# Single-row loads of a graph kernel: one even stream over the loop's slots, 58 row tiles in place of 60

## The chip, the core and the metric

The kernel runs on one core of a Trainium2 chip. A core has five engines, each with its own queue of instructions: TensorE (PE; its weight loads are shown apart as PEld), VectorE (DVE), ScalarE (ACT), GpSimd (POOL) and SyncE (SP). The last issues DMAs and computes nothing; ScalarE and GpSimd issue DMAs too. Engines wait for each other through semaphores. The metric is the time of one execution in microseconds on the device; the median of several runs is compared.

## What is computed

A graph layer with 6,250 nodes of 128 features, 206,250 edges sorted by receiver, and eight heads of 16:

```python
w_ij = silu(edge_feats @ rad_W1 + rad_b1) @ rad_W2 + rad_b2
w_ij = w_ij + (silu(chi_scalar @ sph_W1 + sph_b1) @ sph_W2 + sph_b2)
q_i = (node_feats @ Wq)[receivers]        # 8 heads of 16
k_j = (node_feats @ Wk)[senders]
alpha = (q_i * w_ij * k_j).sum(-1) / sqrt(16) * cutoffs[:, None]
v_j = (node_feats @ Wv)[senders]
out = segment_sum(alpha[..., None] * v_j, receivers) / 16
x = layernorm(x + out)
```

All in float32. The receivers are sorted, so a few neighbouring receivers share each tile; the senders are random, so keys and values have to be fetched edge by edge.

## The kernel before

**Tiles.** An edge tile is 128 edges, one to a partition. Four tiles are a quad (512 edges, 403 quads in all), four quads a group (101 groups). The setup computes keys and values of all nodes and stores them in device memory as `kv_tab`, one row of 1 KB per node. Then the main loop takes one quad per step; a step is called a slot here (`i`), and the quads of a group come in the order 0, 2, 1, 3 (`order`, line 147).

**A slot.** In slot `i` TensorE sums the messages of the group before (L664), computes the hidden layer of quad `i+2` (`first_layers`, L560), brings the queries of quad `i+1` to its edges (`q_at_edges`, L579) and computes the edge weights of quad `i+1` (`weigh`, L612). The last matmul of `q_at_edges` gives TensorE's one signal of the slot. ScalarE's first activation (L597), VectorE's product of query and key (`multiply`, L628) and GpSimd's gathers all wait for such a signal; the gathers issued in slot `i` wait for that of slot `i-1`. VectorE then multiplies by the edge weights (L636), reduces per head (L638) and forms the messages (L653). One reduction at L638 stands for one quad, so counts of quads can be read from it.

**Two ways of fetching keys and values.** Usually GpSimd fetches a tile with one indirect DMA of 128 rows (`gather`, L141): four per quad, issued 14 quads ahead, into a ring of 16 buffers. In 60 quads, spread evenly over quads 14 to 401 (`row_at`, six or seven quads apart), the fourth tile comes in another way: 128 single DMAs of one row each, 60 issued by SyncE and 68 by ScalarE. Such a quad has three gathers. Its fourth tile is a row tile; it lands in a buffer named `wide`, of which there are three in turn. For each DMA the row's byte offset must be in a register, and a load instruction (L208) reads up to 32 of them on SyncE and 24 on ScalarE; so a tile takes two loads on SyncE and three on ScalarE. The DMA itself is at L214. Before `multiply` of such a quad, VectorE waits for the count of all its rows and gathers (L625).

**How the rows are dealt.** `load_rows(i)` stands at the end of each slot. For the tile in turn it puts the rows and loads into a list per engine (`rows_left`), counts a load as `ROW_LOAD` units and a row as one, divides the tile's units over the slots from the previous tile's end to `row_at[k] - ROW_LEAD` (six or seven slots), and lets each engine take as many as it is owed. ScalarE keeps back two units (`ROW_CARRY`), which `copies` issues one by one between the activations of the next slot. SyncE has other work between the rows: node rows (L315), results (L773), receiver numbers (L263) and edge features (L252), one of them in each slot; the first and the last wait for a signal of TensorE two slots back.

Of the kernel before, what the change touches and what calls it, by code (L numbers as in the profile page):

```python
# [14 lines left out]
U8 = mybir.dt.uint8  # L15
# [6 lines left out]
SP = mybir.EngineType.SP  # L22
ACT = mybir.EngineType.Activation
WAIT = mybir.DependencyInfo(mybir.DependencyClass.Sync, mybir.DependencyReason.DATA)

P = 128
# [19 lines left out]
ROW_BYTES = 2 * D * 4  # L46
# [1 line left out]
MSGS = 10  # L48
ACTS = 8
RING = 16  # L50
ROW_TILES = 60
ROW_FIRST = 8
ROW_LAST = 401
ROW_LEAD = 5
ROW_ACT = 68
ROW_AT = {SP: 0, ACT: 64}
ROW_LOAD = 5
ROW_CARRY = 2
ROW_UNITS = {SP: 32, ACT: 24}
XU = 4  # L60
# [3 lines left out]
ROW_SEMS = 8  # L64
# [8 lines left out]
def gnn_kernel(ctx, tc, x, src, dst, weight, edges, rad_W1, rad_b1, rad_W2, rad_b2,  # L73
# [14 lines left out]
    nc = tc.nc  # L88
# [12 lines left out]
    src_x = const.tile([P, math.ceil(XQ / NQ) * GT], I32, name="src_x")  # L101
    at_i = const.tile([ROW_TILES, P + 4], I32, name="at_i")
    scale = const.tile([P, NT], F32, name="scale")
# [33 lines left out]
    def quad_of(name, bufs, width=D):  # L137
        return ep.tile([P, QT, width], F32, name=name, bufs=bufs)
# [8 lines left out]
    order = [g * NQ + j for g in range(NG) for j in (0, 2, 1, 3) if g * NQ + j < QUADS]  # L147
    row_at = [ROW_FIRST + (n + 1) * (ROW_LAST - ROW_FIRST) // ROW_TILES for n in range(ROW_TILES)]
    row_quads = {order[i] for i in row_at}
    row_of = {}  # L150
    row_done = {}
    rows_left = {SP: [], ACT: []}
    owed = {SP: 0, ACT: 0}
    row_work = {}
    row_issued = {}
    row_sems = [tc.alloc_semaphore(f"rows_{n}") for n in range(ROW_SEMS)]
    row_count = [0] * ROW_SEMS
# [4 lines left out]
    def next_rows(engine, n, loads=True):  # L162

        left = rows_left[engine]
        n = min(n, owed[engine])
        while n > 0 and left and (loads or left[0][0] == 1):
            cost, issue = left.pop(0)
            issue()
            n -= cost
            owed[engine] -= cost  # L170
# [19 lines left out]
        kv_of[q] = kv  # L190
        kv_done[q] = kv_sems[at], kv_count[at]

    def load_rows(i):

        k = next((k for k in range(ROW_TILES) if i <= row_at[k] - ROW_LEAD), None)
        start = None if k is None else (row_at[k - 1] if k else ROW_FIRST) - ROW_LEAD + 1
        if k is None or i < start:
            return next_rows(ACT, owed[ACT])
        q = order[row_at[k]]
        slots = row_at[k] - ROW_LEAD + 1 - start  # L200
        table = kv_tab.bitcast(U8).rearrange("(o n) b -> o (n b)", o=1)

        def rows_by(engine, name, a, b):
            regs = {}

            def load(e, m):
                c = ROW_AT[name] + e - a
                regs.update(zip(range(e, e + m), nc.values_load_multi_w_load_instructions(  # L208
                    at_i[k:k + 1, c:c + m], engines=(name,), min_val=0,
                    max_val=(N - 1) * ROW_BYTES,  # L210
                    skip_runtime_bounds_check_because="senders are nodes")[1]))

            def row(p):
                signalled(engine.dma_start(row_of[q][p:p + 1, 0, :].bitcast(U8),  # L214
                                           table[:, ds(regs.pop(p), ROW_BYTES)]))

            items = []
            for e in range(a, b, ROW_UNITS[name]):
                m = min(ROW_UNITS[name], b - e)
                items.append((ROW_LOAD, lambda e=e, m=m: load(e, m)))  # L220
                items += [(1, lambda p=p: row(p)) for p in range(e, e + m)]
            rows_left[name] += items
            return sum(cost for cost, _ in items)

        def signalled(o):
            tc.no_tile_sem_insts.add(o.ins.name)
            tc.add_to_no_dep_group(f"rows_{q}", o.ins)
            o.then_inc(row_sems[k % ROW_SEMS], 16)
            row_count[k % ROW_SEMS] += 16
            row_done[q] = row_sems[k % ROW_SEMS], row_count[k % ROW_SEMS]  # L230
            row_issued[q] = row_issued.get(q, 0) + 1

        n = P - ROW_ACT
        if i == start:
            row_of[q] = quad_of("wide", 3, P)[:, :2, :].rearrange("p t d -> p (t d)")[:, None, :]
            row_work[SP] = rows_by(nc.sync, SP, 0, n)
            row_work[ACT] = rows_by(nc.scalar, ACT, n, P)
        for engine, m in row_work.items():
            a, b = (math.ceil(m * j / slots) for j in (i - start, i - start + 1))
            owed[engine] += b - a  # L240
        next_rows(SP, owed[SP])
        next_rows(ACT, owed[ACT] - ROW_CARRY)

    def kv_parts(q, t):

# [93 lines left out]
    with tc.tile_pool(name="nodes", bufs=1) as nodes, \  # L339
# [76 lines left out]

        rows_f = nodes.tile([P, ROW_TILES], F32, name="rows_f")

# [6 lines left out]
        def turn_rows():  # L425
            pt = nps.tile([P, QT, P], F32, name="pt", bufs=3)
            nc.tensor.transpose(pt[:ROW_TILES, 0, :], rows_f, ident)
            n = P - ROW_ACT
            for a, b, at in ((0, n, ROW_AT[SP]), (n, P, ROW_AT[ACT])):
                nc.vector.tensor_copy(at_i[:, at:at + b - a], pt[:ROW_TILES, 0, a:b])  # L430

# [69 lines left out]
        n = len(chunks)  # L501
# [14 lines left out]
        work = [(k, n) for k, (c, n) in enumerate(chunks)] + [((q, "x"), QT) for q in quads_x]  # L516
        turn(*work[0])
        turn(*work[1])
        for i, (k, n) in enumerate(work):
# [5 lines left out]
            if i >= len(chunks):  # L525
                kv_of[k[0]] = kvs
                a, b = ((j - len(chunks)) * (math.ceil(NT / P) - 1) // XQ for j in (i, i + 1))
# [26 lines left out]
    with tc.tile_pool(name="ps", bufs=1, space=PSUM) as pp, tc.tile_pool(name="loop", bufs=1) as lp:  # L554
# [253 lines left out]
        for g in range(NG - 1):  # L808
            for slot, j in enumerate((0, 2, 1, 3)):
                q = g * NQ + j  # L810
                i = g * NQ + slot
# [63 lines left out]
                if g == NG - 2 and slot == 0:  # L875
                    n = nc.values_load(general, min_val=0, max_val=1)
                if g == NG - 3 and slot in (1, 3):
                    weigh_wide(order[slot // 2 - 3])
                if g == NG - 2 and slot == 1:
                    weigh_wide(order[-1])  # L880
                load_rows(i)
        g, (a, b, c) = NG - 1, order[-3:]
        first_layers(c)
# [224 lines left out]
```

## Time and profile before

| | |
|---|---|
| median of 3 runs | 2596.52 us (2588.82 to 2597.5) |
| the profiled execution | 2599.59 us, of which span 2597.7 us |
| mean granted TensorE clock | 0.837 |
| TensorE matmul busy | 2090.8 us (80%) |
| VectorE busy | 1525.9 us (59%) |
| ScalarE busy | 645.0 us (25%), issue of DMAs not counted |
| GpSimd busy | 1470.8 us (57%) |
| DMA | 307.18 MB, mean 118 GB/s |
| single-row DMAs | 4080 from ScalarE, 3600 from SyncE |
| gathers of 128 rows | 1520 |

How to read it: a group of instructions is given as line, engine, operation, output and inputs, count, then busy time and the mean of one in ns, then the engine's idle time just before them and what ended most of it. "remote" is a release that the profile cannot tie to an instruction, "issue" a stretch in which it sees no wait at all. A `q` behind an engine's name (SPq, ACTq) is its sequencer, which issues DMAs and waits and is not counted as busy. In a listing in order of time the columns are start, duration, engine, line and operation, with the idle time before it in brackets; equal neighbours are merged and counted.

### The profile page before, as it was taken

Reading aid. Unit: us, or ns where it says so; the run is one execution under the profiler, and the core shown is the slowest. Engines: PE = TensorE matmul, PEld = TensorE weight load, DVE = VectorE, ACT = ScalarE, POOL = GpSimd, SP = SyncE. Lnnn points to the kernel's source line nnn. Section 1 sums busy time; section 2 is a strip of 40 time slices with the busy share of each in tenths; the row PEclk is TensorE's granted clock in tenths of the full one; section 3 lists DMA queues with packets and bytes.
Section 4 is the critical chain, followed back from the end, with each engine's and each line's share of the span. In section 5 each row is a group of like instructions: output and inputs, shape, how many; then the busy total and the mean of one; then the engine's idle time right before and its main releaser. Section 6 shows DMA issues by size and latency. Waiting matters only on the chain.

```text
span 2597.7 us, 56700 instructions
## 1 busy us (share of the span) xinstructions
PE 2090.8 (80%) x15990; PEld 1744.9 (67%) x15990; DVE 1525.9 (59%) x3427; ACT 645.0 (25%) x1359; POOL 1470.8 (57%) x1564
## 2 busy tenths in 40 slices
PE   5678888888888788878888878888887888888787
PEld 4567677666767666666667667666766767676666
DVE  3456556656656555656656556555656556565567
ACT  1122222222222222222222222222222222222223
POOL 4456565655565565555556555555555555565540
PEclk7788888888888888888888797888788787887888
DMA  5543444434343343434434434444343343443331
GB/s 180 173 118 112 120 124 116 121 112 122 113 123 116 116 124 114 120 112 122 121 111 123 119 114 121 115 120 121 114 120 118 111 122 115 119 124 108 118 103 35
DMA packets 157219, 307.18 MB, mean 118 GB/s; under 512 B 42022, under 2 KB 91360, under 8 KB 156896
## 3 DMA queue, kind: packets, MB, share of 16 engines
q0 software_dynamic: 73984, 201.43, 27.2%
q1 hardware_dynamic: 72976, 97.35, 11.4%
q10 hardware_dynamic: 9936, 4.72, 0.8%
q8 instruction: 127, 2.08, 0.3%
q14 instruction: 196, 1.61, 0.2%
HBM read 289.88 MB, written 15.11 MB: 117 GB/s over the span
## 4 chain that ended last, share of the span: by engine, by line
PE 38%; issue 20%; SPq 13%; DVE 13%; another core or an unknown queue 10%; ACTq 5%; ACT 1%; DMA 0%; DVEq 0%
PE pw L612 17%; SPq L214 10%; PE pq L579 7%; PE ph L560 6%; ACTq L214 4%; PE po L664 3%; DVE kq L628 3%; DVE side L638 2%; DVE kq L636 2%; SPq L208 2%; PE pq L705 1%; ACT act L597 1%; PE pk L381 1%; PE pq L286 1%
## 5 line engine op out<-in xcount | busy, mean ns | idle before, releaser
L141 POOL DMA_INDIRECT kv<-kv_tab,src_i x1520 | 1436.9, 945 | 1042.9 <-remote 447.9
L612 PE MATMUL pw<-w,act 128*128 128x128 f32 x6448 | 1060.4, 324 | 109.1 <-issue 107.6
L612 PEld LDWEIGHTS pw<-w,act 128*128 128x128 f32 x6448 | 951.7, 231 | 187.0 <-issue 149.7
L597 ACT ACTIVATE act<-ph,b 128x512 f32<-128x512 f32 x806 | 554.7, 689 | 1843.5 <-remote 1374.7
L628 DVE TENSOR_TENSOR kq<-pq,kv 128x512 f32<-128x512 f32 (+1 forms) x404 | 270.6, 670 | 931.3 <-remote 680.0
L560 PE MATMUL ph<-feats,w 32*128 32x512 f32 x1612 | 665.7, 740 | 138.5 <-issue 128.8
L579 PE MATMUL pq<-q,hotT 32*128 32x128 f32 x3224 | 557.5, 321 | 20.9 <-issue 17.8
L579 PEld LDWEIGHTS pq<-q,hotT 32*128 32x128 f32 x3224 | 470.7, 220 | 33.0 <-issue 32.7
L560 PEld LDWEIGHTS ph<-feats,w 32*128 32x128 f32 x1612 | 190.7, 207 | 303.6 <-issue 272.0
L638 DVE TENSOR_REDUCE side<-kq 128x32 f32<-128x512 f32 x404 | 280.2, 694 | 14.0
L653 DVE TENSOR_TENSOR msg<-kv,side 128x512 f32<-128x512 f32 (+1 forms) x404 | 268.7, 665 | 13.9
L636 DVE TENSOR_TENSOR kq<-pw,kq 128x512 f32<-128x512 f32 x404 | 274.1, 679 | 0.0
L664 PE MATMUL po<-msg,hot 128*32 128x128 f32 x3200 | 183.2, 309 | 34.2 <-issue 34.1
L567 PE MATMUL pw<-brow,onesb 3*128 3x512 bf16 x403 | 176.5, 438 | 0.0
L664 PEld LDWEIGHTS po<-msg,hot 128*32 128x32 f32 x3200 | 84.5, 118 | 91.2 <-issue 63.6
L705 PE MATMUL pq<-part,to 128*128 128x128 f32 x196 | 56.6, 380 | 107.6 <-issue 54.4
L705 PEld LDWEIGHTS pq<-part,to 128*128 128x128 f32 x196 | 38.6, 245 | 122.2 <-issue 83.7
L641 DVE TENSOR_TENSOR side<-side,scale 128x32 f32<-128x32 f32 x400 | 79.7, 199 | 13.7
L381 PE MATMUL pk<-wkv,xT 128*128 128x256 f32 x162 | 45.6, 424 | 38.0 <-DVE kv L382 23.9
L292 DVE TENSOR_TENSOR hotT<-relb,side 128x512 f32<-128x512 bf16 x101 | 68.6, 679 | 0.0
L286 PE MATMUL pq<-wq,xT 128*128 128x128 f32 x200 | 49.6, 336 | 23.5 <-issue 15.9
L382 DVE COPY kv<-pk 128x512 f32<-128x512 f32 (+1 forms) x41 | 27.4, 682 | 68.9 <-remote 48.5
(126 smaller groups left out, 892.9 us busy)
## 6 DMA issues: line engine op xcount, KB each, us to landing
wide<-kv_tab ACTq DMA_DIRECT2D x4080, 1.0 KB
wide<-kv_tab SPq DMA_DIRECT2D x3600, 1.0 KB
feats<-in_edges SPq DMA_DIRECT2D x101, 512.0 KB
kv<-kv_tab,src_i POOLq DMA_INDIRECT x1520, 2.9
relb<-rel_four SPq DMA_DIRECT2D x101, 128.0 KB
x<-in_x SPq DMA_DIRECT2D x101, 64.0 KB
out<-y SPq DMA_DIRECT2D x101, 64.0 KB
kv_tab<-kv SPq DMA_DIRECT2D x12, 512.0 KB
```

Of the source, the lines that this page charges most:

```text
L141: return nc.gpsimd.indirect_dma_start(out=o, out_offset=None, in_=table, in_offset=bass.IndirectOffsetOnAxis(ap=index, axis=0))
L214: signalled(engine.dma_start(row_of[q][p:p + 1, 0, :].bitcast(U8), table[:, ds(regs.pop(p), ROW_BYTES)]))
L560: return nc.tensor.matmul(act_of[q, i], w1[r0:r0 + R, :], feats_of[g][r0:r0 + R, c0:c0 + EQ], start=True, stop=True)
L567: nc.tensor.matmul(pw, onesb[f:f + 3, :], brow[f:f + 3].rearrange("p t d -> p (t d)"), start=True, stop=False)
L579: o = nc.tensor.matmul(pq_of[q][:, t, :], hotT_of[g][b, t * P:(t + 1) * P], q_of[g][b, :], start=True, stop=True)
L597: o = nc.scalar.activation(act, act_of[q, i], AF.Silu, bias=b1[:, i:i + 1])
L612: o = nc.tensor.matmul(pw[:, t, :], act_of[q, i][:, t * P:(t + 1) * P], w2[:, i, :], start=False, stop=(t == QT - 1 and i == 1))
L628: o = nc.vector.tensor_tensor(kq_of[q][:, u, :], pq_of[q][:, u, :], kv[:, :, :D], op=OP.mult)
L636: nc.vector.tensor_tensor(m, pw_of[q][:, t, :], m, op=OP.mult)
L638: nc.vector.tensor_reduce(alpha, m.rearrange("p t (h e) -> p t h e", e=HD), AX.X, OP.add)
L653: nc.vector.tensor_tensor(msg_of[q][:, u, :].rearrange("p t (h e) -> p t h e", e=HD), kv[:, :, D:].rearrange("p t (h e) -> p t h e", e=HD) ...
L664: o = nc.tensor.matmul(po_of[g][j * W:(j + 1) * W, :], hot_of[g][:, j * QT + t, :], msg_of[g * NQ + j][:, t, :], start=(t == 0), stop=(t = ...
```

## The change

The rows and loads of all tiles now form one stream. `load_rows(i)` computes how many tiles, as a fraction, are due at slot `i`: (i − 8 + 6) · 58 / 393. Tiles are opened (buffer taken, list filled) in a new function `open_tile` when the stream reaches them, and each engine is owed the difference between what is due by now and what was dealt before. There are 58 row tiles instead of 60, six or seven quads apart (12 of the spacings are six, before 26); two of the quads that had a row tile now have a fourth gather. `ROW_LEAD` goes from 5 to 6, and a load counts as six units instead of five. Behind the last tile ScalarE keeps nothing back.

```diff
-ROW_TILES = 60
+ROW_TILES = 58
 ROW_FIRST = 8
 ROW_LAST = 401
-ROW_LEAD = 5
+ROW_LEAD = 6
-ROW_LOAD = 5
+ROW_LOAD = 6
...
-    def load_rows(i):
-
-        k = next((k for k in range(ROW_TILES) if i <= row_at[k] - ROW_LEAD), None)
-        start = None if k is None else (row_at[k - 1] if k else ROW_FIRST) - ROW_LEAD + 1
-        if k is None or i < start:
-            return next_rows(ACT, owed[ACT])
+    def open_tile(k):
+
         q = order[row_at[k]]
-        slots = row_at[k] - ROW_LEAD + 1 - start
+        row_of[q] = quad_of("wide", 3, P)[:, :2, :].rearrange("p t d -> p (t d)")[:, None, :]
...
         n = P - ROW_ACT
-        if i == start:
-            row_of[q] = quad_of("wide", 3, P)[:, :2, :].rearrange("p t d -> p (t d)")[:, None, :]
-            row_work[SP] = rows_by(nc.sync, SP, 0, n)
-            row_work[ACT] = rows_by(nc.scalar, ACT, n, P)
-        for engine, m in row_work.items():
-            a, b = (math.ceil(m * j / slots) for j in (i - start, i - start + 1))
-            owed[engine] += b - a
+        row_open.append({SP: rows_by(nc.sync, SP, 0, n), ACT: rows_by(nc.scalar, ACT, n, P)})
+
+    def load_rows(i):
+
+        tiles = min(max((i - ROW_FIRST + ROW_LEAD) * ROW_TILES / (ROW_LAST - ROW_FIRST), 0), ROW_TILES)
+        while len(row_open) < math.ceil(tiles):
+            open_tile(len(row_open))
+        for engine in owed:
+            due = sum(min(max(tiles - k, 0), 1) * work[engine] for k, work in enumerate(row_open))
+            owed[engine] += math.ceil(due) - row_dealt[engine]
+            row_dealt[engine] = math.ceil(due)
         next_rows(SP, owed[SP])
-        next_rows(ACT, owed[ACT] - ROW_CARRY)
+        next_rows(ACT, owed[ACT] - (ROW_CARRY if tiles < ROW_TILES else 0))
```

The file is one to three lines shorter behind the edit, so L214 is L211 after it and L597 is L596. Three places show what stands where. SyncE, slots 44 to 47, which begin with the node rows of group 14 (`x`); before:

```order
L315 DMA x<-in_x 128x512
L214 DMA wide<-kv_tab 1x1024 x8
L773 DMA out<-y_2251 128x512
L214 DMA wide<-kv_tab 1x1024 x10
L263 DMA relb<-rel_four 128x1x512
L214 DMA wide<-kv_tab 1x1024 x10
L252 DMA feats<-in_edges 128x1024
L208 TENSOR_LOAD at_i
L214 DMA wide<-kv_tab 1x1024 x7
```

and now:

```order
L314 DMA x<-in_x 128x512
L211 DMA wide<-kv_tab 1x1024 x4
L205 TENSOR_LOAD at_i
L772 DMA out<-y_2295 128x512
L211 DMA wide<-kv_tab 1x1024 x11
L262 DMA relb<-rel_four 128x1x512
L211 DMA wide<-kv_tab 1x1024 x11
L251 DMA feats<-in_edges 128x1024
L211 DMA wide<-kv_tab 1x1024 x6
```

The other work of a slot stands where it stood; the rows between it are a few more or fewer, and the loads of row numbers fall elsewhere. GpSimd, the gathers of the quads 59 to 66 of the order, a row per quad (numbers of buffers in the names); before:

```order
L141 DMA kv_5510<-kv_tab_60,src_i_67 128x256 x4
L141 DMA kv_5627<-kv_tab_60,src_i_67 128x256 x3
L141 DMA kv_5752<-kv_tab_60,src_i_67 128x256 x4
L141 DMA kv_5862<-kv_tab_60,src_i_67 128x256 x4
L141 DMA kv_5938<-kv_tab_60,src_i_67 128x256 x4
L141 DMA kv_6112<-kv_tab_60,src_i_67 128x256 x4
L141 DMA kv_6179<-kv_tab_60,src_i_67 128x256 x4
L141 DMA kv_6289<-kv_tab_60,src_i_67 128x256 x3
```

and now:

```order
L141 DMA kv_5487<-kv_tab_60,src_i_67 128x256 x4
L141 DMA kv_5557<-kv_tab_60,src_i_67 128x256 x4
L141 DMA kv_5670<-kv_tab_60,src_i_67 128x256 x4
L141 DMA kv_5794<-kv_tab_60,src_i_67 128x256 x3
L141 DMA kv_5903<-kv_tab_60,src_i_67 128x256 x4
L141 DMA kv_5974<-kv_tab_60,src_i_67 128x256 x4
L141 DMA kv_6146<-kv_tab_60,src_i_67 128x256 x4
L141 DMA kv_6212<-kv_tab_60,src_i_67 128x256 x4
```

The quads with three gathers come a little less often. ScalarE, the slot whose quad time has three gathers (slot 45 before, slot 47 now; `part` and `tot` are copies of the running sums, `y` is a result); before:

```order
L597 ACTIVATE act_105<-ph,b_73 128x512
L214 DMA wide<-kv_tab 1x1024
L709 ACTIVATE tot<-pq 128x128
L214 DMA wide<-kv_tab 1x1024
L597 ACTIVATE act_106<-ph,b_73 128x512
L742 ACTIVATE y_4026<-y_4026,shift,rs 128x128
L214 DMA wide<-kv_tab 1x1024
L208 TENSOR_LOAD at_i
L214 DMA wide<-kv_tab 1x1024 x6
```

and now:

```order
L596 ACTIVATE act_101<-ph,b_73 128x512
L211 DMA wide<-kv_tab 1x1024
L699 ACTIVATE part<-po 128x128
L211 DMA wide<-kv_tab 1x1024
L596 ACTIVATE act_102<-ph,b_73 128x512
L741 ACTIVATE y_4018<-y_4018,shift,rs 128x128
L211 DMA wide<-kv_tab 1x1024 x11
```

Nine rows and a load stood in that slot; thirteen rows and no load stand there now.

More of the change, by code (lines that the diff above doesn't have):

```diff
@@ L153, in gnn_kernel @@
     owed = {SP: 0, ACT: 0}
-    row_work = {}
+    row_dealt = {SP: 0, ACT: 0}
+    row_open = []
     row_issued = {}
@@ L213, in row @@
             def row(p):
-                signalled(engine.dma_start(row_of[q][p:p + 1, 0, :].bitcast(U8),
-                                           table[:, ds(regs.pop(p), ROW_BYTES)]))
+                o = engine.dma_start(row_of[q][p:p + 1, 0, :].bitcast(U8),
+                                     table[:, ds(regs.pop(p), ROW_BYTES)])
+                tc.no_tile_sem_insts.add(o.ins.name)
+                tc.add_to_no_dep_group(f"rows_{q}", o.ins)
+                o.then_inc(row_sems[k % ROW_SEMS], 16)
+                row_count[k % ROW_SEMS] += 16
+                row_done[q] = row_sems[k % ROW_SEMS], row_count[k % ROW_SEMS]
+                row_issued[q] = row_issued.get(q, 0) + 1
             items = []
@@ L223, in rows_by @@
             return sum(cost for cost, _ in items)
[L225 to L231, printed above, removed]
-        n = P - ROW_ACT
-        if i == start:
-            row_of[q] = quad_of("wide", 3, P)[:, :2, :].rearrange("p t d -> p (t d)")[:, None, :]
-            row_work[SP] = rows_by(nc.sync, SP, 0, n)
-            row_work[ACT] = rows_by(nc.scalar, ACT, n, P)
-        for engine, m in row_work.items():
-            a, b = (math.ceil(m * j / slots) for j in (i - start, i - start + 1))
-            owed[engine] += b - a
+        n = P - ROW_ACT
+        row_open.append({SP: rows_by(nc.sync, SP, 0, n), ACT: rows_by(nc.scalar, ACT, n, P)})
[7 more added lines that the diff above has]
+            row_dealt[engine] = math.ceil(due)
         next_rows(SP, owed[SP])
-        next_rows(ACT, owed[ACT] - ROW_CARRY)
+        next_rows(ACT, owed[ACT] - (ROW_CARRY if tiles < ROW_TILES else 0))
     def kv_parts(q, t):
```

## The prediction

> **What bounds the kernel now.** I read the page first, then the time order of GpSimd, then SyncE and VectorE at the quads with a row tile, and last the same rows in an early and a late stretch. The page's groups and its chain:
>
> ```profile
> span 2597.7 us, 56700 instructions
> PE pw L612 17%; SPq L214 10%; PE pq L579 7%; PE ph L560 6%; ACTq L214 4%; PE po L664 3%; DVE kq L628 3%; DVE side L638 2%; DVE kq L636 2%; SPq L208 2%; PE pq L705 1%; ACT act L597 1%; PE pk L381 1%; PE pq L286 1%
> L141 POOL DMA_INDIRECT kv<-kv_tab,src_i x1520 | 1436.9, 945 | 1042.9 <-remote 447.9 <-issue 352.0 <-PE pq L579 170.8
> L597 ACT ACTIVATE act<-ph,b 128x512 f32<-128x512 f32 x806 | 554.7, 689 | 1843.5 <-remote 1374.7
> ```
>
> No engine is full, and yet SyncE's issue of single rows (L214) is a tenth of the chain. GpSimd in order of time shows the beat. First an ordinary quad, then a quad with three gathers, then the rows that ScalarE issued in that short quad:
>
> ```profile
> 454.83 0.94 POOL L141 DMA_INDIRECT kv<-kv_tab,src_i  x1 [1.62 <-remote]
> 456.08 0.95 POOL L141 DMA_INDIRECT kv<-kv_tab,src_i  x1 [0.30 <-issue]
> 457.33 0.95 POOL L141 DMA_INDIRECT kv<-kv_tab,src_i  x1 [0.31 <-issue]
> 458.59 0.95 POOL L141 DMA_INDIRECT kv<-kv_tab,src_i  x1 [0.31 <-issue]
> 461.09 0.94 POOL L141 DMA_INDIRECT kv<-kv_tab,src_i  x1 [1.55 <-remote]
> ...
> 521.96 0.94 POOL L141 DMA_INDIRECT kv<-kv_tab,src_i  x1 [1.53 <-remote]
> 524.46 0.95 POOL L141 DMA_INDIRECT kv<-kv_tab,src_i  x1 [0.30 <-issue]
> 526.73 0.94 POOL L141 DMA_INDIRECT kv<-kv_tab,src_i  x1 [1.32 <-remote]
> ```
>
> ```profile
> 521.73 0.69 ACT L597 ACTIVATE act<-ph,b 128x512 f32<-128x512 f32 x1 [4.42 <-remote]
> 522.75 0.69 ACT L597 ACTIVATE act<-ph,b 128x512 f32<-128x512 f32 x1
> 522.82 3.51 ACTq L214 DMA_DIRECT2D wide<-kv_tab  x10
> 526.49 0.69 ACT L597 ACTIVATE act<-ph,b 128x512 f32<-128x512 f32 x1 [3.06 <-remote]
> ```
>
> Gathers start 1.25 us apart, and after each burst GpSimd, ScalarE and VectorE wait for TensorE's one signal, 1.3 to 1.6 us. Four gathers make a quad of 6.26 us (454.83 to 461.09), three make one of 4.77 us (521.96 to 526.73). So the number of gathers sets the beat. Now a late quad that takes its fourth tile from single rows:
>
> ```profile
> 2343.29 4.67 SPq L214 DMA_DIRECT2D wide<-kv_tab  x11
> 2349.36 0.56 DVE L628 TENSOR_TENSOR kq<-pq,kv 128x384 f32<-128x384 f32 x1 [6.97 <-issue]
> 2347.40 0.95 POOL L141 DMA_INDIRECT kv<-kv_tab,src_i  x1 [0.30 <-issue]
> 2354.82 0.94 POOL L141 DMA_INDIRECT kv<-kv_tab,src_i  x1 [6.47 <-PE pq L579]
> ```
>
> SyncE's last row of the tile goes out at 2347.96, VectorE has stood idle 6.97 us and starts 1.4 us later, TensorE gets the product's bank late, and GpSimd's next burst waits 6.47 us where 1.5 is usual. It was not always so. The last rows of an early tile, its use, and the same at the tile ten further on:
>
> ```profile
> 296.37 3.90 SPq L214 DMA_DIRECT2D wide<-kv_tab  x9
> 327.98 0.56 DVE L628 TENSOR_TENSOR kq<-pq,kv 128x384 f32<-128x384 f32 x1 [1.50 <-remote]
> 714.92 4.01 SPq L214 DMA_DIRECT2D wide<-kv_tab  x7
> 722.77 0.56 DVE L628 TENSOR_TENSOR kq<-pq,kv 128x384 f32<-128x384 f32 x1 [0.97 <-remote]
> ```
>
> The lead falls from 27.7 us (300.27 to 327.98) to 3.8 us (718.93 to 722.77) in 65 quads. SyncE cannot keep up with the rows; from there on it sets the mean pace. VectorE's waits in the late stretch (us in total, times, longest) say the same, as do the quads counted by their reductions in both stretches (206 to 723 and 723 to 2515 us):
>
> ```profile
> DVE kq L628 <- remote: 496.6, 202, 3.0
> DVE kq L628 <- DVEq L625: 48.0, 11, 6.4
> DVE kq L628 <- DMA wide<-kv_tab: 43.8, 8, 7.1
> DVE kq L628 <- issue: 30.9, 5, 7.0
> L638 DVE TENSOR_REDUCE side<-kq 128x32 f32<-128x512 f32 x85 | 59.1, 695 | 2.9
> L638 DVE TENSOR_REDUCE side<-kq 128x32 f32<-128x512 f32 x288 | 200.1, 695 | 10.0
> L141 POOL DMA_INDIRECT kv<-kv_tab,src_i x327 | 309.2, 945 | 207.6 <-remote 103.0 <-issue 75.2 <-PE pq L579 24.5
> L141 POOL DMA_INDIRECT kv<-kv_tab,src_i x1112 | 1051.2, 945 | 741.8 <-remote 332.3 <-issue 256.6 <-PE pq L579 136.8
> ```
>
> 517/85 = 6.08 us a quad early, 1792/288 = 6.22 late.
>
> **The change part by part.** (a) *The stall that can go.* 0.14 us a quad over 288 quads is 40 us. Two other readings bound it. GpSimd's idle time per gather rises from 207.6/327 = 0.635 to 741.8/1112 = 0.667 us, times 1112 is 36 us. VectorE's 24 waits for rows (48.0 + 43.8 + 30.9 = 122.7 us), less an ordinary wait of 496.6/202 = 2.46 us each, are 64 us. I take 40, the reading of the whole pace; ends 36 and 64.
>
> (b) *Does SyncE keep up now?* Need before: 60 rows per tile, 60 tiles on 393 slots, 9.16 rows a quad. After: 58 tiles, 8.855 rows a quad. Supply in the early stretch: ten tiles (600 rows) between the two ends above, 418.7 us, are 1.433 rows/us, times 6.08 us is 8.71 rows a quad. SyncE also loads row numbers twice a tile:
>
> ```profile
> L208 SPq TENSOR_LOAD <-at_i x120: 420/1932/2442, 137.9 to 2559.1; - x120
> ```
>
> Four loads fewer (two tiles at two) free 0.02 us a quad, 0.03 rows; the lower share of short quads adds about 0.01 row. Supply 8.75. The shortfall shrinks from 0.45 to 0.105 rows a quad, 0.073 us; over 393 quads 29 us, and the lead to be eaten is 27.7 us. So the rows become late only at the very end, if at all. A missing row cost 0.14/0.45 = 0.31 us. I take 1 us for what stays. Ends: nothing, and with 1% less supply a shortfall of 0.195 rows, which uses the lead up after 204 quads and costs 189 × 0.195 × 0.31 = 11 us.
>
> Two edits that the words of the change put first count for nothing in (b). "Six slots ahead" moves SyncE's end hardly at all: the old code deals a tile's last row in slot row_at − 5, the new one when the stream passes the tile, which by its formula is 4 to 5 slots before the multiplication, against 4; ScalarE gains one slot and was never late. And the even deal cannot help a queue that is behind, since it works through its entries in order anyway; it only spares ScalarE the slots with 14 rows. What brings the balance is the two tiles left out: 120 of 3,600 rows on SyncE.
>
> (c) *Two gathers more.* Two quads grow from three gathers to four: 2 × (6.26 − 4.77) = 3 us; by the 1.25 us between starts alone 2.5. I take 3.
>
> (d) *At nothing.* 136 fewer rows on ScalarE, at 3.51/10 = 0.35 us each 48 us of its queue: it idles 1374.7 us for TensorE's signal. If it were the bound instead of GpSimd, they would be a gain. Two pairs of 128-wide products on VectorE become parts of wider ones inside its 2.46 us waits, and two fewer conversions in the setup are a fraction of a microsecond. The new tiles' buffer (three of them) is written some seven slots after its last reader, so SyncE's first row of a tile waits no more than now; nothing that stands behind it (feature blocks, node rows, outputs) is held.
>
> Sum: −40 + 1 + 3 = −36 us. The profiled execution took 2599.6 us (2597.7 of it span), so 2563.6; it lies 3.1 us above the median of the runs, 2596.5, so 2560.5, said as 2561.
>
> One rule speaks to (b). SyncE's rows are quick in parts of a quad and slow in others; here four take 2.87 us although ScalarE issues only two beside them and then nothing until 1018.76:
>
> ```profile
> 1015.65 2.87 SPq L214 DMA_DIRECT2D wide<-kv_tab  x4
> 1015.67 0.55 ACTq L214 DMA_DIRECT2D wide<-kv_tab  x2
> 1018.76 0.69 ACT L597 ACTIVATE act<-ph,b 128x512 f32<-128x512 f32 x1 [5.04 <-remote]
> ```
>
> The Trainium skill, "Perfetto Trace Analysis", section "DMA Instruction — HWDGE (DVE, Sync)", has the descriptor generator shared by two issuing engines and locked for one at a time, the lock wait being part of the profiled time. By that SyncE would lose a fixed time per tile to ScalarE's rows and not a fixed time per quad; its late need, 1792 us for 2637/60 = 44 tiles or 40.7 us a tile, would fit well into 6.776 quads of 6.08 us, (b) would be 0 and the sum 1 us lower. The trace does not bear it out as the main cause, since the slow rows fall where ScalarE issues none.
>
> **The rivals.** *SyncE stays late.* Its supply is known from one stretch. At 2.4% less, 8.5 rows a quad, the shortfall is 0.355 rows, 0.25 us; the lead is gone after 112 quads, and 281 × 0.355 × 0.31 = 31 us of the stall stay: 2599.6 − 40 + 31 + 3 − 3.1 = 2590.5. For it: the lead's loss of 23.9 us over 65 quads, 0.37 us a quad, is a little more than 0.45 rows at 1.433 rows/us make (0.31). Against it, the late stretch, in which SyncE never rested:
>
> ```profile
> L214 SPq DMA_DIRECT2D wide<-kv_tab x2637: 2/218/837, 722.9 to 2512.7; - x189
> ```
>
> 2637/288 = 9.16 rows a quad of 6.22 us; that is 1.47 rows/us, not less than the early rate.
>
> *ScalarE becomes the bound, slower than before.* In the new order 41 of 57 short quads meet 12 or 13 of ScalarE's rows; in the old one 53 of 59 met 7 or 9 and a load of row numbers. In the quad at 521.73 the activations and the first two rows take 1.09 us; eleven more at 0.35 us make 4.95 us, more than the 4.77 of a short quad. If that overrun held TensorE up, the short quads would lose their gain: 41 × 1.49 us is 61 us, 2561 + 61 = 2622. It decides once the second activation, done at 523.44 in that quad, moves some 3 us towards the signal at 526.49. Against it: that quad has 12 rows, the last of them out at 526.33, and the signal comes on time; one row more is 0.2 us late, and the next quad has 6.2 us to take it up.
>
> *All of the waits count.* If the 64 us of (a) come back: 2599.6 − 64 + 1 + 3 − 3.1 = 2536.5. Against it: the pace of the whole says 40.
>
> **How the numbers follow.** The forecast has 0.72; its own range is 2535 to 2575 from the ends of (a), (b) and (c), its likely part 2548 to 2572. SyncE late has 0.14, ScalarE 0.06, the full waits 0.08. A measurement of this kernel tells a change from none at about 0.3%, 7.8 us, so 2588.7 to 2604.3 is "the same". Faster: 0.72 + 0.08 + a little over half of 0.14 = 0.88. The same: the rest of SyncE late, 0.06. Slower: ScalarE, 0.06. The range leaves out ScalarE's case, the slow end of the first rival and part of the full waits: 2540 to 2586.
>
> **What would show it right or wrong.** GpSimd's quads should stay at 6.2 and 4.8 us with 1522 gathers; VectorE's waits for rows and for the row semaphore (L625 before) should go from 24 in the late stretch to a handful; the pace between 723 us and the last gathers should be 6.08 to 6.10 us a quad; SyncE's lead at a tile's use should shrink slowly over the whole run and not reach 4 us before its last fifth. The prediction is wrong if VectorE still idles 4 to 7 us at every second tile, if short quads last over 5.5 us with ScalarE as what ends the wait, or if SyncE, while it is behind, issues under 1.43 rows/us.

## The result and the profile after

The changed kernel takes 2564.78 us (median of four runs, 2562.05 to 2569.25), the kernel before 2596.61 us beside it (2588.82 to 2597.5). The ratio is 0.9882, 95% interval 0.9859 to 0.9905: faster by 1.2%. 2561 was predicted, with a range of 2540 to 2586. The profiled execution took 2569.25 us, of which span 2567.5. Its page, in the rows that answer to those of before:

```profile
span 2567.5 us, 56170 instructions
SPq L211 21%; PE pw L611 10%; SPq L205 4%; PE pq L578 4%; PE ph L559 4%; ACTq L211 2%; DVE kq L627 2%; DVE side L637 2%; PE po L663 2%; DVE kq L635 2%; PE pk L380 1%; SPq L772 1%; SPq L314 1%; SPq L262 1%
L141 POOL DMA_INDIRECT kv<-kv_tab,src_i x1522 | 1442.3, 948 | 1009.5 <-remote 490.3
L596 ACT ACTIVATE act<-ph,b 128x512 f32<-128x512 f32 x806 | 554.6, 689 | 1813.9 <-remote 1551.1
```

SyncE's rows (SPq L211) have a larger share of the chain than before, 21% against 10%, although the kernel is faster. The chain is one path followed back from the end; along it SyncE is still the late engine wherever a tile's rows are late. What such waits cost is read from VectorE. Its waits before the product of query and key in the late stretch, 723 to 2485 us, just before the last gathers (total, times, longest):

```profile
DVE kq L627 <- remote: 553.4, 229, 3.0
DVE kq L627 <- DVEq L624: 43.1, 9, 6.9
DVE kq L627 <- DMA wide<-kv_tab: 5.4, 2, 3.6
DVE kq L627 <- issue: 5.2, 4, 2.8
```

Before, 24 waits for rows took 122.7 us; now it is 15 waits and 53.7 us. Less an ordinary wait of 553.4/229 = 2.42 us each, 17 us of stall are left of 64. Seven of the 15 are no longer than ordinary waits, so this sum is low. Only eight belong to late tiles, 3.6 to 6.9 us long and 43.3 us together, where 21 of the 24 did before, with 118.6 us; by these alone 24 us of stall are left of 67. The reductions and gathers in the two stretches 206 to 723 and 723 to 2485 us give the pace:

```profile
L637 DVE TENSOR_REDUCE side<-kq 128x32 f32<-128x512 f32 x85 | 59.1, 695 | 2.9
L637 DVE TENSOR_REDUCE side<-kq 128x32 f32<-128x512 f32 x288 | 200.1, 695 | 9.9
L141 POOL DMA_INDIRECT kv<-kv_tab,src_i x328 | 310.9, 948 | 207.6 <-remote 106.3 <-issue 73.9 <-PE pq L578 20.1
L141 POOL DMA_INDIRECT kv<-kv_tab,src_i x1111 | 1052.8, 948 | 708.6 <-remote 365.2 <-issue 257.8 <-PE pq L578 70.2
```

Early it is 517/85 = 6.08 us a quad as before. Late it is 1762/288 = 6.12, where it was 6.22. The 288 late quads took 1762 us instead of 1792: these 30 us are the whole gain of the profiled execution (2599.6 to 2569.3). The granted clock of TensorE was 0.85 in both early stretches, 0.84 in the late one before and 0.85 now. A part of the gain through the clock is not excluded, but the waits of the late tiles alone fell by more than 30 us.

The rows still fall late, only later in the run. SyncE's last rows of an early tile with that tile's use, and the same 22 tiles on, in order of time:

```profile
258.44 1.15 SPq L211 DMA_DIRECT2D wide<-kv_tab  x3
294.41 0.56 DVE L627 TENSOR_TENSOR kq<-pq,kv 128x384 f32<-128x384 f32 x1 [1.41 <-remote]
...
1190.74 1.09 SPq L211 DMA_DIRECT2D wide<-kv_tab  x4
1195.62 0.56 DVE L627 TENSOR_TENSOR kq<-pq,kv 128x384 f32<-128x384 f32 x1 [0.99 <-remote]
```

The lead shrinks from 34.8 us (259.59 to 294.41) to 3.8 us (1191.83 to 1195.62). In these 22 tiles SyncE issued 1320 rows in 932.2 us, 1.416 a microsecond. The uses lie 901.2 us apart, 22 · 393/58 = 149 quads of 6.05 us. So SyncE supplied 8.56 rows a quad where 8.855 are wanted, and lost 0.21 us a quad. Behind that point some tiles are late, as here:

```profile
1645.10 4.79 SPq L211 DMA_DIRECT2D wide<-kv_tab  x9
1651.04 0.95 POOL L141 DMA_INDIRECT kv<-kv_tab,src_i  x1 [0.30 <-issue]
1651.94 0.56 DVE L627 TENSOR_TENSOR kq<-pq,kv 128x384 f32<-128x384 f32 x1 [6.12 <-DVEq L624]
1655.73 0.95 POOL L141 DMA_INDIRECT kv<-kv_tab,src_i  x1 [3.75 <-issue]
```

VectorE stands for 6.12 us, and GpSimd's next burst begins 3.75 us after the last instead of 1.5.

### The profile page after: what moved, and what is told of

It reads as the page before. It is cut to its first block, busy times and chain, and to the rows that moved or that the text cites. A ratio compares the mean times of both kernels' runs of the same rounds, so it can differ in the third digit from the quotient of the medians.

```text
span 2567.5 us, 56170 instructions
## 1 busy us (share of the span) xinstructions
PE 2077.4 (81%) x15990; PEld 1728.2 (67%) x15990; DVE 1526.2 (59%) x3421; ACT 643.5 (25%) x1359; POOL 1476.3 (57%) x1566
## 4 chain that ended last, share of the span: by engine, by line
SPq 29%; issue 25%; PE 23%; DVE 10%; another core or an unknown queue 9%; ACTq 3%; DMA 1%; ACT 1%; DVEq 0%
SPq L211 21%; PE pw L611 10%; SPq L205 4%; PE pq L578 4%; PE ph L559 4%; ACTq L211 2%; DVE kq L627 2%; DVE side L637 2%; PE po L663 2%; DVE kq L635 2%; PE pk L380 1%; SPq L772 1%; SPq L314 1%; SPq L262 1%
## 5 line engine op out<-in xcount | busy, mean ns | idle before, releaser
L611 PE MATMUL pw<-w,act 128*128 128x128 f32 x6448 | 1045.9, 322 | 92.7 <-issue 91.3
L611 PEld LDWEIGHTS pw<-w,act 128*128 128x128 f32 x6448 | 939.4, 228 | 169.4 <-issue 131.0
L596 ACT ACTIVATE act<-ph,b 128x512 f32<-128x512 f32 x806 | 554.6, 689 | 1813.9 <-remote 1551.1
L578 PE MATMUL pq<-q,hotT 32*128 32x128 f32 x3224 | 548.6, 317 | 4.4 <-issue 4.4
L578 PEld LDWEIGHTS pq<-q,hotT 32*128 32x128 f32 x3224 | 462.8, 217 | 9.5 <-issue 9.3
L663 PE MATMUL po<-msg,hot 128*32 128x128 f32 x3200 | 188.4, 310 | 42.4 <-issue 41.9
L296 DVE TENSOR_TENSOR hot<-rel,side 128x512 f32<-128x512 f32 x100 | 67.9, 679 | 0.0
```

The lines of the kernel that those rows point to most:

```text
L578: o = nc.tensor.matmul(pq_of[q][:, t, :], hotT_of[g][b, t * P:(t + 1) * P], q_of[g][b, :], start=True, stop=True)
L596: o = nc.scalar.activation(act, act_of[q, i], AF.Silu, bias=b1[:, i:i + 1])
L611: o = nc.tensor.matmul(pw[:, t, :], act_of[q, i][:, t * P:(t + 1) * P], w2[:, i, :], start=False, stop=(t == QT - 1 and i == 1))
L663: o = nc.tensor.matmul(po_of[g][j * W:(j + 1) * W, :], hot_of[g][:, j * QT + t, :], msg_of[g * NQ + j][:, t, :], start=(t == 0), stop=(t = ...
```

## The experiments

All runs are of one core, on three chips, and ratios are to the kernel before on the same chip. The first four runs ("old deal" to "56 rows on SyncE") share one chip and the next four a second; there the kernel before takes 2646 and 2638 us. The last four share a third, where it takes 1973 us. That difference became the last question. The expectations in microseconds were meant for the kernel before at 2597 us, so they are compared by ratio.

**The old deal with 58 tiles.** The change's table size alone, in the code of before:

```diff
-ROW_TILES = 60
+ROW_TILES = 58
```

> The kernel before with 58 row tiles and nothing else changed (old dealing, lead 5, a load counted as 5). Theory A, SyncE's row rate decides: it must issue 8.86 rows a quad whichever way they are dealt, so the time is that of the changed kernel, 2560 to 2572 us, with late rows only in the second half. Theory B, the even stream or the sixth slot of lead decides: at most 10 us of the 32 come from two tiles fewer, 2584 to 2600 us.

2603.8 us, ratio 0.985 (0.9823 to 0.9877): the whole gain of the change, without the stream and without the sixth slot.

**The stream with 60 tiles.** The other half, in the changed kernel:

```diff
-ROW_TILES = 58
+ROW_TILES = 60
```

> The changed kernel with 60 row tiles again. Theory A: SyncE needs 9.16 rows a quad and can do some 8.6, so the rows are late from about a third of the run as in the kernel before: 2586 to 2600 us. Theory B (the stream or the lead decides): 2558 to 2568 us, since two gathers fewer save 3 us.

2645.54 us, ratio 1.0009 (0.9986 to 1.0033): nothing. VectorE's waits before the product, over the whole run:

```profile
DVE kq L627 <- DVEq L624: 113.1, 23, 10.8
DVE kq L627 <- issue: 27.9, 5, 6.9
DVE kq L627 <- DMA wide<-kv_tab: 27.7, 7, 5.7
```

35 waits and 168.7 us for rows. An even stream keeps SyncE late just the same when the stream is too long. Less an ordinary wait of 693.9/276 = 2.51 us each (its waits ended by "remote"), the stall is 81 us, more than the 64 of the first profile.

**56 tiles.** Two tiles fewer again: 56 · 60/393 = 8.55 rows a quad on SyncE, what it supplied above.

```diff
-ROW_TILES = 58
+ROW_TILES = 56
```

> The changed kernel with 56 row tiles. Theory A: SyncE needs 8.55 rows a quad, about what it does; the 18 us of stalls at late tiles that the changed kernel still shows go, and two more gathers cost 3 us: 2547 to 2554 us. If the remaining stalls have another cause than SyncE's rate: 2566 to 2570 us.

2574.24 us, ratio 0.9751 (0.9719 to 0.9784), the best of the runs on these two chips. The same view of its whole run:

```profile
DVE kq L627 <- remote: 835.2, 335, 5.8
DVE kq L627 <- PE pq L578: 61.4, 37, 6.2
DVE kq L627 <- ACT act L596: 2.9, 1, 2.9
DVE kq L627 <- PE pw L611: 2.8, 1, 2.8
```

No wait for rows is left, though GpSimd has one gather more for every tile less. The gain is larger than theory A had it (2547 to 2554 us, 0.981 to 0.984): on this chip there was more stall to take away, as the run before shows.

**56 rows on SyncE, 72 on ScalarE.** 58 tiles as in the change, but only 58 · 56/393 = 8.26 rows a quad on SyncE (the table of row numbers gets wider, so that ScalarE's part ends inside it):

```diff
-ROW_ACT = 68
+ROW_ACT = 72
-    at_i = const.tile([ROW_TILES, P + 4], I32, name="at_i")
+    at_i = const.tile([ROW_TILES, P + 8], I32, name="at_i")
```

> The changed kernel with 4 of the 60 SyncE rows of each tile given to ScalarE (56 and 72), same gathers. Theory A: SyncE needs 8.27 rows a quad, no tile is late, 2543 to 2551 us. Rival: ScalarE, with 4 rows (1.4 us) more per tile, becomes the bound or the descriptor generator shared with SyncE takes the gain back: 2562 us or more.

2581.62 us, ratio 0.9766 (0.9743 to 0.9789), and no tile late. This, too, is more than theory A had (0.979 to 0.982). It is SyncE's row count that matters, not the number of tiles, and four rows more per tile on ScalarE do no harm.

**The change once more**, unchanged, on the second chip, as the base for the next three.

> The changed kernel unchanged, as the base for the runs beside it on the same chip: 0.984 to 0.989 of the kernel before, late tiles in the second half only.

2604.58 us, ratio 0.9863 (0.9824 to 0.9903). The interval overlaps that of the first measurement. The first late tile comes at 1128 us, before half of the run, and 13 tiles are late; "in the second half only" was not met.

**Nine slots ahead.** A longer lead to eat from:

```diff
-ROW_LEAD = 6
+ROW_LEAD = 9
```

> The changed kernel with a lead of 9 slots in place of 6. Theory A: SyncE's shortfall of 0.1 to 0.2 us a quad stays, but it has three slots, 18.6 us, more to eat up, so lateness sets in some 100 quads later or not at all: 5 to 15 us below the changed kernel on the same chip. If lead does nothing (a tile's rows wait for something else, such as their buffer): within 3 us of it, and tiles as late as there.

2597.12 us, ratio 0.9833 (0.9791 to 0.9875), 7.5 us below the run before it, with overlapping intervals. The waits on the row count of this kernel, behind those of the change on the same chip:

```profile
DVE kq L627 <- DVEq L624: 62.0, 17, 8.7
```

```profile
DVE kq L627 <- DVEq L624: 8.2, 2, 5.4
```

A lead is a stock that is used up once. It moves the first late tile back, from 1128 to 1666 us, but the rate stays what it was: SyncE issues 1402 rows between 600 and 1600 us with it and 1403 without.

**64 rows on SyncE.** The suspected cost made larger, 58 · 64/393 = 9.45 rows a quad:

```diff
-ROW_ACT = 68
+ROW_ACT = 64
```

> The changed kernel with 4 rows of each tile moved from ScalarE to SyncE (64 and 64), same gathers. Theory A: SyncE needs 9.44 rows a quad, more than the 9.16 of the kernel before, so late from the first third on, and some 25 us above the kernel before: 1.006 to 1.016 of it. Rival, the number of tiles decides and not SyncE's rows: 0.984 to 0.990 as the changed kernel.

2679.8 us, ratio 1.0151 (1.0108 to 1.0195): slower than before, with the same number of tiles and gathers as the changed kernel. VectorE's waits for the row count alone:

```profile
DVE kq L627 <- DVEq L624: 174.0, 29, 12.0
```

Four rows a tile decide between 1.4% faster and 1.5% slower.

**SyncE alone.** What slows SyncE's rows: ScalarE's rows, or GpSimd's gathers? 30 tiles, all 128 rows from SyncE, none from ScalarE, the gathers as always:

```diff
-ROW_TILES = 58
+ROW_TILES = 30
-ROW_ACT = 68
-ROW_AT = {SP: 0, ACT: 64}
+ROW_ACT = 0
+ROW_AT = {SP: 0, ACT: 128}
-            for a, b, at in ((0, n, ROW_AT[SP]), (n, P, ROW_AT[ACT])):
+            for a, b, at in ((0, n, ROW_AT[SP]),):
```

> 30 row tiles, all 128 rows of each issued by SyncE, none by ScalarE (9.77 rows a quad for SyncE); 28 gathers more than the changed kernel, some 42 us. What is read is SyncE's rate while it is behind. If its slow stretches come from GpSimd's gathers: 1.35 to 1.5 rows/us as in all runs so far, the lead eaten up within 70 quads and late tiles from then on. If they come from sharing the descriptor generator with ScalarE's rows: over 1.8 rows/us, SyncE keeps up and no tile is late.

One run, 2609.19 us. SyncE kept up with 30 · 128/393 = 9.77 rows a quad: no tile is late. Its rows between 600 and 1600 us, first here, then in the change on the same chip:

```profile
L211 SPq DMA_DIRECT2D wide<-kv_tab x1560: 2/224/1364, 599.7 to 1599.1; - x195
```

```profile
L211 SPq DMA_DIRECT2D wide<-kv_tab x1403: 2/202/1464, 599.7 to 1599.2; - x176
```

Without ScalarE's rows it issues at least 1.56 rows a microsecond, against 1.40 with them. What it could do at most does not show, since it was never behind. But something other than ScalarE's rows still holds it. The move of each row's offset into place, an instruction of its own before the DMA, takes anything from 2 to 1257 ns; from 2540 us on, behind the last gather, it takes 29 to 38:

```profile
L211 SPq MOVE wide<-kv_tab x1559: 2/29/1257, 601.8 to 1599.1; - x195
L211 SPq MOVE wide<-kv_tab x64: 29/29/38, 2540.0 to 2564.8; - x64
```

In the changed kernel, too, SyncE is quick behind the last gathers, where ten rows take 3.21 us:

```profile
2497.00 3.21 SPq L211 DMA_DIRECT2D wide<-kv_tab  x10
```

The outcome lies between the two theories. By this one run ScalarE's rows cost SyncE time on this chip, and so does something that ends with the gathers; that it is the gathers themselves is not shown.

**On the third chip: 56 tiles again, and two further divisions.** 62 tiles with 54 and 74 rows, and 60 tiles with 56 and 72, keep SyncE at 8.52 and 8.55 rows a quad with fewer gathers:

```diff
-ROW_TILES = 58
+ROW_TILES = 62
-ROW_ACT = 68
+ROW_ACT = 74
-ROW_UNITS = {SP: 32, ACT: 24}
+ROW_UNITS = {SP: 32, ACT: 25}
```

```diff
-ROW_TILES = 58
+ROW_TILES = 60
-ROW_ACT = 68
+ROW_ACT = 72
```

(the table of row numbers is wider in both).

> The kernel with 56 tiles once more, beside the three kernels of this call. A (SyncE keeps up, the gathers set the beat): ratio to the kernel before 0.972 to 0.978, no tile for which VectorE idles over 3.2 us. If the gain of the earlier run belonged to its chip: over 0.982.

> 62 tiles, 54 rows of each by SyncE and 74 by ScalarE: SyncE has 8.52 rows a quad of the order, ScalarE 11.7 (10.0 in the changed kernel, 9.7 with 56 tiles). A (SyncE's rows decide, ScalarE has room): SyncE keeps up as with 56 tiles (8.55), no late tile, and six gathers fewer at 1.45 us each take 9 us off: 0.003 below the kernel with 56 tiles, so 0.969 to 0.975. Rival (ScalarE's rows become the bound): 74 rows in 6.34 quads, 12 to 14 of them in a short quad; short quads last 5.1 us or more instead of 4.9, VectorE or TensorE wait for ScalarE's activation, and the ratio is over 0.978.

> 60 tiles as in the kernel before, but 56 rows by SyncE and 72 by ScalarE: 8.55 rows a quad on SyncE, 11.0 on ScalarE. A (the number of rows on SyncE decides, not the number of tiles): no late tile, four gathers fewer than with 56 tiles, ratio 0.970 to 0.977, against 1.001 for 60 tiles with 60 rows on SyncE. Rival (ScalarE): over 0.980, short quads longer than 5.1 us.

None of the gains came. On this chip the kernel before takes 1973.04 us (1971.95 to 1973.32, seven runs), that with 56 tiles 1971.75, ratio 0.9993 (0.9979 to 1.0007), and that with 60 tiles 1977.84, ratio 1.0024 (1.001 to 1.0039). So the gain of the 56 tiles does not hold on every chip; it was seen on the first. The changed kernel itself was not run on this one.

The kernel with 62 tiles takes 2555.28 us, ratio 1.2954 (1.2936 to 1.2972). The loads of row numbers (minimum, median, maximum in ns), with 62 tiles and then with 60:

```profile
L205 ACTq TENSOR_LOAD <-at_i x186: 1906/5566/6047, 81.0 to 2503.1; - x186
```

```profile
L205 ACTq TENSOR_LOAD <-at_i x180: 1662/1802/2027, 81.2 to 1928.9; - x180
```

In units of 25 the second and third load of a tile begin at the numbers 89 and 114 of the table's row; in units of 24 they begin at 88 and 112. Those from 89 and 114 take 5.4 to 6.0 us, those from 88 and 112 take 1.8, and ScalarE's activations stand behind them. The first load of each tile with 62 tiles reads 25 numbers, too, but in 2 us, so it is not the count; that it is the start was not tested apart. These 124 loads at some 3.8 us more are 470 us of the 577 by which the kernel is longer than that with 60 tiles (spans 2552.3 and 1975.3); the rest is not accounted for. The test of ScalarE's rows as the bound is spoilt, and what was meant as a better version is none.

**34 tiles from SyncE alone**, more than it could do, to see its full rate:

```diff
-ROW_TILES = 58
+ROW_TILES = 34
-ROW_ACT = 68
+ROW_ACT = 0
```

> 34 tiles whose 128 rows all come from SyncE; ScalarE issues none. 11.07 rows a quad are asked of SyncE, more than it can do, so its true rate without ScalarE's rows shows. With the kernel of 30 tiles it kept up with 9.8 rows a quad at 0.485 us a row. A (the gathers slow SyncE's rows by themselves, ScalarE's rows add a smaller part): SyncE falls behind, 0.44 to 0.49 us a row, 1.6 to 1.75 rows/us, and VectorE idles for late tiles from the first half on. Rival (the 0.485 us was slack, only ScalarE's rows slow SyncE): 0.36 us a row, over 1.9 rows/us, the lead never used up.

One run on the third chip, 2081.61 us. SyncE's rows between 600 and 1600 us, and VectorE's waits for the row count over the whole run:

```profile
L211 SPq DMA_DIRECT2D wide<-kv_tab x2190: 227/228/422, 599.9 to 1599.4; - x200
```

```profile
DVE kq L627 <- DVEq L624: 426.9, 32, 17.4
```

2.19 rows a microsecond is the rival's rate, and still the lead was used up from the first tiles on, as theory A had it: the quads are shorter on this chip, so the rows are wanted faster. Neither is decided by it for the first two chips.

**One kernel, two chips.** The program with 56 tiles ran on the first chip and on the third, and can be laid side by side. SyncE's row instructions between 600 and 1600 us (the move of the offset, the DMA; minimum, median, maximum in ns), first chip, then third:

```profile
L211 SPq MOVE wide<-kv_tab x1390: 2/29/865, 599.7 to 1599.2; - x199
L211 SPq DMA_DIRECT2D wide<-kv_tab x1390: 2/203/820, 600.4 to 1600.0; - x199
```

```profile
L211 SPq MOVE wide<-kv_tab x1772: 29/29/38, 600.9 to 1597.5; - x197
L211 SPq DMA_DIRECT2D wide<-kv_tab x1772: 224/228/460, 601.0 to 1597.6; - x197
```

On the third chip the move takes 29 to 38 ns; on the first it takes anything from 2 to 865, though the median is 29 on both. There SyncE is held for a while and then runs its instructions in a bunch. The slow pace alone does not do it, nor does a low clock alone: in the kernel with 62 tiles, 2552.3 us long on the third chip at a granted clock of 0.829, the move takes 29 to 38 ns as well. Now a piece of each in order of time, again the first chip and then the third (the matmuls that give the signal, gathers, and what waits for the signal):

```profile
1001.27 0.60 PE L578 MATMUL pq<-q,hotT 32*128 32x128 f32 x4
1003.21 0.95 POOL L141 DMA_INDIRECT kv<-kv_tab,src_i  x1 [0.30 <-issue]
1003.82 5.57 SPq L211 DMA_DIRECT2D wide<-kv_tab  x10
1005.42 0.69 ACT L596 ACTIVATE act<-ph,b 128x512 f32<-128x512 f32 x1 [4.38 <-remote]
1005.42 0.69 DVE L627 TENSOR_TENSOR kq<-pq,kv 128x512 f32<-128x512 f32 x1 [2.70 <-remote]
1005.65 0.94 POOL L141 DMA_INDIRECT kv<-kv_tab,src_i  x1 [1.50 <-remote]
```

```profile
1007.16 1.06 PE L578 MATMUL pq<-q,hotT 32*128 32x128 f32 x4
1008.26 0.95 POOL L141 DMA_INDIRECT kv<-kv_tab,src_i  x1 [0.30 <-issue]
1008.29 0.69 ACT L596 ACTIVATE act<-ph,b 128x512 f32<-128x512 f32 x1 [4.46 <-issue]
1008.74 3.25 SPq L211 DMA_DIRECT2D wide<-kv_tab  x10
1009.51 0.94 POOL L141 DMA_INDIRECT kv<-kv_tab,src_i  x1 [0.30 <-issue]
```

On the third chip the activation starts 0.07 us after the matmuls' end (1008.22 to 1008.29), in the middle of the gathers, GpSimd never pauses, and ten rows take 3.25 us. On the first the matmuls end at 1001.87, and activation, product and next burst all start at 1005.4 to 1005.7, together, some 1.3 us after the burst's last gather ended at 1004.16; ten rows take 5.57 us. So on the first chip something holds the signal and SyncE while GpSimd gathers, and the scattered moves of the second look the same. The gathers' idle time over the run is 1015.9 us there and 465.0 here, 551 us of the 604 between the two spans (2573.8 and 1969.7):

```profile
L141 POOL DMA_INDIRECT kv<-kv_tab,src_i x1524 | 1442.2, 946 | 1015.9 <-remote 549.1 <-issue 345.7 <-PE pq L578 53.9
```

```profile
L141 POOL DMA_INDIRECT kv<-kv_tab,src_i x1524 | 1442.2, 946 | 465.0 <-issue 404.2 <-DVE kq L627 13.5 <-DVEq L624 9.2
```

What holds them was not found. Each chip was measured at one time only, so a property of the chip and a state that it was in are not told apart. One candidate is the recording itself: the Trainium skill, "NOTIFIC — the notification-queue block", section "Overflow: three behaviours, one of which stalls the engine", says that in one of its modes a full queue of records stalls the engine that writes them. No run here was without a record, so this stays open. By the profiles both of the kernels whose times were to be predicted ran on chips that behave like the first: their signals come behind the bursts.

## Why the prediction was right

**The bounds.** GpSimd's beat and SyncE's lateness were what the changed kernel answers to. With the rows on SyncE at 9.45, 9.16, 8.86 and 8.55 a quad, the ratio is 1.015, 1.001, 0.986 and 0.975 (64 rows, 60 tiles, the change, 56 tiles); the first three have late tiles and the last has none. The wait of 1.3 to 1.6 us after each burst, which the prediction took as a given of the kernel, is one of the chip. That the result fell on a chip with this wait is luck: on the third, where it is missing, the kernels with 56 tiles and with 56 rows on SyncE, both without a late tile, gained nothing.

**(a) The stall that can go** held: of the 40 us that the late stretch lost against the early pace, 30 came back, and of the 67 in VectorE's waits for late tiles, 43.

**(b) What stays late** is the step that was mis-sized. It was put at 1 us, with 11 as its far end; measured are 0.036 us a quad against the early pace times 288, 10 us. GpSimd's idle time per gather (708.6/1111 = 0.638 us late, 0.633 early) says 5 us, VectorE's waits for late tiles 24. The mechanism was right, and its price of the right size: 8.855 − 8.56 = 0.295 rows a quad are missing, over the some 210 quads behind 1195 us, at 0.31 us each, 19 us. The supply was wrong: 8.75 rows a quad had been worked out from ten tiles of one stretch (8.71) and 0.04 for fewer loads; 8.56 were measured over 22 tiles. The lead was therefore gone at tile 25 of 58, at 47% of the run, and not in its last fifth. The case that 2.4% less supply would give, the first rival's, is nearer to what happened in its rate (8.5) than the forecast's, but not in its price: its 31 us did not come, since 0.295 rows were missing and not 0.355, and since the early tiles had 34.8 us of lead and not 27.7. The prediction had the hint in hand: the lead's loss of 0.37 us a quad, named there for the rival, is 0.53 rows and a supply of 8.63. It was weighed as a chance instead of being put into the sum. The total came out close because this term is small beside (a).

**(c) Two gathers more**: 1522 were counted, as forecast. The step is too small to be told from the runs.

**(d) and the two edits at nothing.** The old deal with 58 tiles gains 1.5%, the stream with 60 tiles nothing: "what brings the balance is the two tiles left out" is shown. That six slots "moves SyncE's end hardly at all" is not quite so: the lead of the early tiles grew by about 6 us, one slot. A slot is worth little, by the run with nine 7.5 us for three.

**The rule on the shared generator.** The prediction held that the trace does not bear it out as the main cause. Without ScalarE's rows SyncE kept up with 9.77 rows a quad on the second chip, where the change supplied too little for 8.855 on the same chip. So, by that one run, ScalarE's rows do slow SyncE there, and the prediction dismissed too much. On the third chip ten rows take 3.25 us with ScalarE's rows and the gathers beside them, about what they take in the changed kernel once the gathers have ended (3.21 us), so no lock wait of any size is to be seen there. What ScalarE's rows cost is thus no fixed price of sharing; whether the rule's lock wait is how they cost it on the second chip is not shown.

**The signs named beforehand.** GpSimd's quads stayed, 6.22 us with four gathers and 4.87 with three (medians between 206 and 2480 us; 6.24 and 4.78 before). VectorE's 24 waits were to become a handful and became 15, eight of them for late tiles, at about every fourth tile behind 1195 us and not at every second; the late pace was to be 6.08 to 6.10 us and is 6.12; the lead was to last for four fifths of the run and lasted not half. While it is behind, SyncE was not to issue under 1.43 rows a microsecond; from 1277 to 2485 us it issues 1.44:

```profile
L211 SPq DMA_DIRECT2D wide<-kv_tab x1742: 2/205/820, 1279.4 to 2484.8; - x194
```

So the three signs that missed all missed on the side of (b).

**The rivals.** ScalarE as the bound did not come: 72 rows of each tile on ScalarE, at 58 tiles, cost nothing that the ratio shows (0.9766). All 64 us of waits back would have needed no late tile. By the pace of the late stretch the sum is −40 + 10 = −30 us, against −30.3 measured and −36 forecast; this is the gain read once more and not a second proof. The 10 us hold whatever the two gathers of (c) cost there, so (c) is not added again; the forecast's +1 and +3 stand against them, and the 6 us between are the miss of (b).

## What to carry to other kernels

A queue that is short of its demand by a few per cent looks healthy until its lead is used up; so compare the lead at use early and late in the run, and cut the demand below the measured supply, with a margin wider than the uncertainty of a rate taken from one stretch. An even deal or a longer lead only moves the moment. Before tuning a balance of a per cent, look at the shortest instruction of a queue (a register move): where its duration scatters, the engine is being held, and a balance found there may gain nothing on a chip where it does not scatter.

## What the runs showed of the hardware

The same program took 2574 us on one chip and 1972 us on another, with the mean granted TensorE clock at 0.846 and 0.93. In the pieces shown, TensorE's signal takes effect on the first only about 1.3 us after a burst of gathers, and ten of SyncE's rows take 5.57 us instead of 3.25; SyncE's register moves take 2 to 865 ns there and 29 to 38 on the other. On the third chip four gathers follow each other at 1.25 us without a pause, and GpSimd's 1524 gathers, 1442.2 us busy and 465.0 us between them, nearly fill the run. The load of 24 or 25 registers takes 1.8 us from the numbers 88 and 112 of a row in one kernel and 5.6 us from 89 and 114 in another.
